# A macaron layer in fp32: row additions off VectorE, and its small work regrouped within the attention units

## The chip, the cores and the metric

The kernel runs on one core of a Trainium2 chip. A core has five engines that run side by side, each with its own instruction queue: TensorE (PE in the profile; its weight loads are PEld), VectorE (DVE), ScalarE (ACT), GpSimd (POOL) and SyncE (SP, which here only issues DMAs). The metric is the time of one execution on the device in microseconds (us); lower is better. Before the change the median of three runs is 1375.16 us (1372.16 to 1376.97).

## What is computed

Tokens come as x of shape 8 x 1024 x 256 in fp32. The layer is

```
x = x + 0.5 * moe(layernorm(x))     # 8 experts, top 2, capacity 1.25 N / E = 1280
x = x + attention(layernorm(x))     # 16 heads of 16, causal, softmax, with Wq, Wkv, Wo and biases
x = x + 0.5 * moe(layernorm(x))
```

An expert that more tokens choose than its capacity is dropped as a whole (keep = counts <= cap, and 2 N choices over 8 experts average 2048). The kernel therefore computes gates, top-2 choices and counts for both expert layers while it does the attention, and branches to code for the expert layers only if some expert fits. With these inputs that code is not run: the time is the time of the attention with the two gates beside it.

## The kernel before, in words

The function `attention` (L686 on) handles 8 batches of 1024 tokens. A batch has four head groups of four heads each; one head group of one batch is a **unit** u, 32 in all, with b, g = divmod(u, 4). The text below calls the four units of a batch g = 0, 1, 2, 3. A unit has 24 **steps**, k = 0 to 23 (loop at L1237). In each step TensorE computes, interleaved,

- two blocks of exponent scores of unit u (`sc`, `e_steps`): ScalarE takes their exp into `pT`, GpSimd zeroes the part above the diagonal with an affine select where the block lies on it, and two or three steps later TensorE multiplies them with the values (`pav`, `values`, L927);
- two blocks of the same scores of unit u + 1 in the other orientation (`sm`, `m_steps`, L852), of which only the row maximum is wanted. Each block is read by VectorE: in steps 0 to 7 and 16 to 23 by a reduction with the causal mask, recorded as `CUSTOM_DVE_ANT_0` and `DVE_READ_ACCUMULATOR2_ANT`, whose sizes run 512, 512, 384, 384, 256, 256, 128, 128 columns; in steps 8 to 15 by a plain `TENSOR_REDUCE` of 512 columns into `first`.

All `sc` and `sm` blocks take turns on six PSUM banks (`score`, L700): a step asks for four, in the order sc, sm, sc, sm. A bank is free for the next block once ScalarE or VectorE has read it. So the second `sm` block of a step can start only when VectorE has read the first `sm` block of the step before.

Everything else is done beside these steps by generators held in `Beside` (L53 on). A generator yields a number (go on so many steps later), or PIECE, QK or REST (go on where TensorE has room for a piece of work). Those that matter here:

- `prepare(b)` (L732) loads a batch and takes layernorm statistics tile by tile with `ln_stats` (`bn_stats`, `bn_aggr`); `enter(b)` normalises on GpSimd (`xn_a`) and transposes.
- `values_of` (L774): per tile of 128 tokens one product `pv` with 264 columns, 256 values and 8 gate logits. ScalarE copies the values to `vaug`, VectorE the logits.
- `leave(b, hf)` (L974): half a batch leaves the attention. Per tile a product `px` with 264 columns; VectorE adds it to the residual row in `xa`; the statistics of the new row are queued in `light`, one taken per step; then the half goes to HBM. It runs in the units g = 0 and g = 1 of the next batch.
- `residual(b)`: four GpSimd additions of the output bias to the residual. `gate_first(b)` and `regate(b)`: the choices (`choose`, L339) for the first and the second expert layer, 20 or 21 small VectorE instructions with one exp on ScalarE, spread over steps by `yield 1`.

Instructions on TensorE, VectorE, ScalarE and GpSimd are kept in the order in which the code issues them (`InOrder`, L27): an instruction that waits holds up everything behind it on its engine. SyncE's DMAs wait in their own order.

Before unit 0 there is an **opening** (L1130 on): x of batch 0 and the weights are loaded, statistics are taken, GpSimd computes the reciprocal deviation `rstd_a`, two halves are normalised, transposed and projected (`project`, L823, which packs heads with eight DMAs per half), and the `sm` blocks of unit 0 run alone. At the **end** (L1290) the last half of batch 7 leaves and the last counts decide the branch.

Of the kernel before, what the change touches and what calls it, by code (L numbers as in the profile page):

```python
# [10 lines left out]
F32 = mybir.dt.float32  # L11
# [91 lines left out]
def macaron_kernel(  # L103
# [112 lines left out]
    def weights(pool, bank, matmul, transpose):  # L216
# [18 lines left out]
        gpsimd.tensor_scalar(bkqT[64:], bkqT[64:], QSCALE, None, ALU.mult)  # L235

# [102 lines left out]
    def choose(rp, tag, n, lg):  # L339
        def new(name, shape=(P, n, E), dt=F32):  # L340
            return rp.tile(list(shape), dt, tag=f"{name}{n}", name=f"{name}_{tag}")

        def over_e(a):
            return a.unsqueeze(2).to_broadcast([P, n, E])

        mx = new("mx", (P, n))
        vector.tensor_reduce(mx, lg, AX.X, ALU.max)
        lc = new("lc")
        vector.tensor_tensor(lc, lg, over_e(mx), ALU.subtract)
        prob = new("prob")  # L350
        yield 1
        scalar.activation(prob, lc, AF.Exp)
        yield 1
        cand = new("cand")
        ohs = [new(f"oh{k}") for k in range(2)]

        def lowest(oh):
            vector.tensor_tensor(cand, cand, iota_e.unsqueeze(1).to_broadcast([P, n, E]), ALU.add)
            first = new("first", (P, n))
            vector.tensor_reduce(first, cand, AX.X, ALU.min)  # L360
            vector.tensor_tensor(oh, cand, over_e(first), ALU.is_equal)

# [12 lines left out]
        vector.scalar_tensor_tensor(key, key, 1e30, lc, ALU.mult, ALU.min)  # L375
        vector.scalar_tensor_tensor(key, ohs[0], -1e32, key, ALU.mult, ALU.add)
        yield 1
        best = new("best", (P, n))
        vector.tensor_reduce(best, key, AX.X, ALU.max)
        vector.tensor_tensor(cand, key, over_e(best), ALU.is_equal)  # L380
        yield 1
        vector.tensor_scalar(cand, cand, -100.0, None, ALU.mult)
        lowest(ohs[1])
        yield 1
        return prob, ohs
# [300 lines left out]
    def attention(run_no, src, dst, gate0, logits, tally):  # L686
# [3 lines left out]
        with stack:  # L690
# [41 lines left out]
            def prepare(b):  # L732
                xb = xbs[b] = ap.tile([P, TB, D + E], F32, tag="xa", name=f"xa{b}", bufs=3)
                nc.sync.dma_start(out=xb[:, :, :D], in_=src[b].rearrange("(j p) d -> p j d", p=P))
                yield 2
                st, mv = ln_tiles(f"a{b}")
                for j in range(TB):
                    ln_stats(xb, j, st, mv)
                    yield 2
                stds[b] = norm.tile([P, TB], F32, tag="std", name=f"std{b}")  # L740
                lns[b] = mv, ln_rstd(mv, f"a{b}", stds[b])
                yield 2
# [31 lines left out]
            def values_of(b, apart, j0=0, j1=TB):  # L774
# [7 lines left out]
                for j in range(j0, j1):  # L782
# [16 lines left out]
                    vector.tensor_copy(lg[:, j, :], pv[:, D : D + E])  # L799
# [23 lines left out]
            def project(u, parts=(0, 512)):  # L823
                b, g = divmod(u, NG)
                xnT = xnTs[b]
                for s0 in parts:
# [17 lines left out]
                    for k in range(8):  # L844
                        r = 32 * (k % 4)
                        nc.sync.dma_start(  # L846
# [125 lines left out]


            def leave(b, hf):  # L974
# [28 lines left out]
                for i in range(TB // 2):  # L1003
# [13 lines left out]
                    vector.tensor_tensor(xb[:, j, :], px[:, : D + E], xb[:, j, :], ALU.add)  # L1017
                    light.append(lambda j=j: ln_stats(xb, j, *gate_lns[b]))
# [84 lines left out]
            def regate(b, j0, j1):  # L1103
# [5 lines left out]
                yield 3  # L1109
# [34 lines left out]
            for qT in qTs:  # L1144
                gpsimd.memset(qT, 0.0)
            for vaug in vaugs:
                gpsimd.memset(vaug[:, :, : NH * VW].rearrange("p t (h r) -> p t h r", r=VW)[:, :, :, HD:], 1.0)
                gpsimd.memset(vaug[:, :, NH * VW :], 1.0)
# [9 lines left out]
            for j0 in (0, HT):  # L1158
                for j in range(j0, j0 + HT):
                    ln_stats(xb, j, st, mv)  # L1160
                part = slice(j0, j0 + HT)
                rstds.append(ln_rstd(mv[:, part, :], f"a0_{j0}", stds[0][:, part]))
            for hf in range(2):
# [12 lines left out]
            owed, light, last, ons = deque(), deque(), [], {}  # L1176
# [3 lines left out]
            for u in range(-1, NU):  # L1180
                b, g = divmod(u, NG)
                if u == 0:
                    beside.finish(opening)
                    preparing = beside.add(prepare(1))
                    opening = beside.add(values_of(0, 0, HT, TB), first=True)
                    projecting = beside.add(project(2))
                    beside.add(chain((PIECE,), turning, residual(0), gate_first(0)))
# [3 lines left out]
                if u >= 0 and g == 3 and b + 1 < B:  # L1191
                    beside.finish(valuing)
                    valuing = beside.add(chain(values_of(b + 1, 0, HT, TB), residual(b + 1)))
# [4 lines left out]
                if g == 3 and u >= 0:  # L1198
                    if b + 2 < B:
                        preparing = beside.add(prepare(b + 2))  # L1200
# [13 lines left out]
                for k in range(0, STEPS, 2) if u == NU - 1 else ():  # L1214
# [10 lines left out]
                    if k == 0:  # L1225
                        beside.add(divided(b, 1, 8, 12, ons[1][:, 1], (1, 3, 3, 3)))
                    if k == 0:
# [9 lines left out]
                for k in range(STEPS) if 0 <= u < NU - 1 else ():  # L1237
# [14 lines left out]
                    if light:  # L1252
# [8 lines left out]
                    if g == 0 and b and k == 9:  # L1261

                        beside.add(gate_first(b))
                    if g == 0 and b and k == 2:
                        beside.add(chain(leave(b - 1, 1), regate(b - 1, 0, TB)))
# [25 lines left out]
            for k, _ in enumerate(leave_last(B - 1, 1, last.pop(), (scalar.copy, vector.tensor_copy))):  # L1291
                for _ in range(3 if k < 2 else len(beside.works) * STEPS):
# [66 lines left out]
```

## Time and profile before

| what | value |
|---|---|
| median of 3 runs | 1375.16 us |
| the profiled execution | 1375.38 us, of it span 1373.6 us |
| TensorE busy | 1336.6 us (97%) |
| VectorE busy | 1038.2 us (76%) |
| ScalarE busy | 785.5 us (57%) |
| GpSimd busy | 398.1 us (29%) |
| residual additions on VectorE (`xa<-px`) | 64 of 427 ns |
| logit copies on VectorE (`logits<-pv`) | 64 of 159 ns |
| statistics on VectorE (`st_a`, `st_g`; `mv_a`, `mv_g`) | 128 of 420 ns; 128 of 182 ns |

The span runs from the first to the last instruction of the core. A busy share is the time in which at least one instruction of the engine is under way. Matmuls overlap and their ends are modelled, so an interval counted as busy for TensorE can still hold a wait. A chain of waits follows the work that ended last back to what released it.

### The profile page before, as it was taken

To read this page: it belongs to the slowest core of one execution; us is meant where nothing else is said; L and a number is where in the kernel's file an instruction comes from. 1 tells how busy PE (TensorE), PEld (TensorE's weight loads), DVE (VectorE), ACT (ScalarE), POOL (GpSimd) and SP (SyncE) were. 2 spreads that over 40 slices of the span, in tenths; PEclk is the share of its full clock that TensorE was granted. 3 is DMA by queue.
4 is the path that set the end of the run, shared out by engine and by line. 5 is a ranking of instruction groups with operands and counts; after the bars stand their busy time and mean duration, and the time that the engine had idled before them with its cause. 6 is when DMAs were issued, how large, how long until landed. Compare 5 with 4: busy or idle time off the path is not lost.

```text
span 1373.6 us, 51244 instructions
## 1 busy us (share of the span) xinstructions
PE 1336.6 (97%) x20664; PEld 445.5 (32%) x20664; DVE 1038.2 (76%) x3417; ACT 785.5 (57%) x1790; POOL 398.1 (29%) x720
## 2 busy tenths in 40 slices
PE   6999999999999999999999999999999999999994
PEld 2333333333333333333333333333333333333331
DVE  3877677887787877877788777788777787787854
ACT  3256665565655565556665656656665556555562
POOL 3034114341235213152141411424123521312321
PEclk9899999999999999999999999999999999999997
DMA  4011111121121211212021211212112111121101
GB/s 142 18 27 42 42 43 56 55 72 42 53 65 49 83 31 48 74 52 77 21 58 60 84 46 37 60 57 73 42 54 58 53 49 34 50 74 42 60 27 34
DMA packets 67024, 73.73 MB, mean 54 GB/s; under 512 B 24688, under 2 KB 42232, under 8 KB 66776
## 3 DMA queue, kind: packets, MB, share of 16 engines
q1 hardware_dynamic: 65688, 69.82, 17.4%
q8 instruction: 165, 2.70, 0.8%
q14 instruction: 83, 0.68, 0.2%
q10 hardware_dynamic: 1088, 0.53, 0.1%
HBM read 26.87 MB, written 26.20 MB: 39 GB/s over the span
## 4 chain that ended last, share of the span: by engine, by line
PE 95%; DVE 3%; DMA 1%; issue 1%; POOL 0%; ACT 0%; SPq 0%; ACTq 0%; POOLq 0%
PE sc L37 42%; PE pav L37 24%; PE sm L37 10%; PE pq L37 9%; PE pv L37 5%; PE px L37 4%; PE pta L37 1%; DVE sm L37 1%; DMA bkqT<-in_L_attn_bq_dram 0%; DVE cand_g L37 0%; SPq L846 0%; PE px_last L37 0%; DVE top L37 0%; DVE first_g L37 0%; DVE oh_g L37 0%
## 5 line engine op out<-in xcount | busy, mean ns | idle before, releaser
L37 ACT ACTIVATE pT<-sc 128x512 f32<-128x512 f32 (+3 forms) x1536 | 668.9, 488 | 518.1 <-PE sm L37 381.4
L37 PE MATMUL sm<-kT,qT 32*64 32x512 f32 (+3 forms) x6144 | 752.8, 510 | 4.2 <-DVE top L37 2.2
L37 PE MATMUL sc<-qT,kT 32*64 32x512 f32 (+3 forms) x6144 | 693.8, 507 | 0.0
L37 DVE TENSOR_REDUCE first<-sm 128x1 f32<-128x512 f32 x512 | 328.7, 685 | 123.3 <-PE sm L37 122.6
L37 POOL TENSOR_SCALAR_AFFINE_SELECT pT<-pT 128x256 f32<-128x256 f32 x512 | 207.6, 408 | 735.4 <-ACT pT L37 734.9
L37 PE MATMUL pav<-pT,vaug 128*32 128x256 f32 (+2 forms) x5120 | 381.8, 370 | 2.2 <-POOL pT L37 1.5
L37 DVE CUSTOM_DVE_ANT_0 sm<-sm,causal 128x256 f32<-128x256 f32 (+3 forms) x512 | 241.8, 514 | 90.8 <-PE sm L37 80.3
L37 DVE CUSTOM_DVE_ANT_0 sm<-sm,causal,first 128x256 f32<-128x256 f32 (+3 forms) x512 | 261.4, 556 | 54.3 <-PE sm L37 48.5
L37 PEld LDWEIGHTS sc<-qT,kT 32*64 32x64 f32 x6144 | 183.1, 130 | 345.9 <-ACT pT L37 266.8
L37 PEld LDWEIGHTS sm<-kT,qT 32*64 32x64 f32 x6144 | 210.8, 130 | 33.4 <-DVE top L37 21.5
L37 PEld LDWEIGHTS pav<-pT,vaug 128*32 128x32 f32 x5120 | 102.5, 108 | 362.3 <-issue 282.7
L37 DVE DVE_READ_ACCUMULATOR2_ANT top<- 128x1 f32 x1024 | 145.5, 142 | 0.0
L37 PE MATMUL pq<-xnT,wkqT 128*32 128x512 f32 x1024 | 136.5, 608 | 1.3 <-ACT xnT L37 1.3
L37 PE MATMUL pv<-wvT,xnT 128*32 128x264 f32 x1024 | 81.1, 391 | 0.0
L37 PE MATMUL px<-woT,on 128*32 128x264 f32 x960 | 76.3, 390 | 0.0
L37 POOL TENSOR_SCALAR xn_a<-xa,mv_a,rstd_a 128x256 f32<-128x256 f32 x56 | 67.5, 1221 | 0.0
L37 ACT ACTIVATE packed<-pq,bkqT 128x512 f32<-128x512 f32 x64 | 45.4, 710 | 11.7 <-PE pq L37 11.7
L37 POOL TENSOR_TENSOR xa<-xa,bo_all 128x528 f32<-128x528 f32 x32 | 41.8, 1308 | 14.3 <-issue 13.7
L37 POOL TENSOR_TENSOR on<-on,inv 128x512 f32<-128x512 f32 (+1 forms) x32 | 40.3, 1282 | 14.1 <-DMA inv<-inv_d 14.1
L37 PEld LDWEIGHTS pq<-xnT,wkqT 128*32 128x32 f32 x1024 | 25.9, 110 | 55.5 <-issue 52.0
L37 PEld LDWEIGHTS pv<-wvT,xnT 128*32 128x32 f32 x1024 | 29.6, 110 | 41.8 <-ACT att L37 18.9
L37 PEld LDWEIGHTS px<-woT,on 128*32 128x32 f32 x960 | 27.3, 109 | 37.3 <-ACT att L37 11.4
(122 smaller groups left out, 430.8 us busy)
## 6 DMA issues: line engine op xcount, KB each, us to landing
att_d<-att SPq DMA_DIRECT2D x62, 256.0 KB
kT<-packed SPq DMA_DIRECT2D x256, 32.0 KB
qT<-packed SPq DMA_DIRECT2D x256, 32.0 KB
out_dram<-xa SPq DMA_DIRECT2D x16, 512.0 KB
on<-att_d SPq DMA_DIRECT2D x30, 256.0 KB
inv<-inv_d SPq DMA_DIRECT2D x30, 256.0 KB
xa<-in_L_attn_x_dram SPq DMA_DIRECT2D x7, 1024.0 KB
xa<-in_L_attn_x_dram SPq DMA_DIRECT2D x2, 512.0 KB
```

Of the source, the lines that this page charges most:

```text
L37: i = call(*args, **kwargs)
```

## The change

1. `leave`: ScalarE copies `px` to a tile `row` in SBUF (4 buffers), and GpSimd adds it to `xa`, one tile per step in steps 8 to 16, or when the half leaves. The statistics are queued once the addition is issued and taken only in steps 8 to 15 of g = 1 and g = 2.
2. `values_of`: ScalarE copies the logits.
3. The small work gets units of its own, and steps 8 to 15: `prepare` of batch 2 and later waits 32 steps after its load and then takes a tile a step (in g = 0); `gate_first(b)` moves from g = 0, k = 9 to g = 3, k = 8 of its batch (batch 7: the last unit); `regate(b - 1)` moves from behind the second `leave` to g = 2, k = 9; `residual(b)` moves from g = 3 of the batch before to g = 0, k = 9. `choose` and `regate` lose one and two waiting steps.
4. Opening: GpSimd's scaling of the bias `bkqT`, three of four fills of `qT` and the fills of `vaug` move behind the two `rstd_a`; four of the eight packing DMAs per half of unit 0 are issued by ScalarE.
5. End: the last `leave_last` lets fewer steps of other work pass (1 instead of 3 at its first stop).

TensorE's instructions stand in the same order before and after.

```diff
-        gpsimd.tensor_scalar(bkqT[64:], bkqT[64:], QSCALE, None, ALU.mult)
...
         scalar.activation(prob, lc, AF.Exp)
-        yield 1
...
-            def prepare(b):
+            def prepare(b, wait, apart):
...
-                yield 2
+                yield wait
                 st, mv = ln_tiles(f"a{b}")
                 for j in range(TB):
                     ln_stats(xb, j, st, mv)
-                    yield 2
+                    yield apart
...
-                    vector.tensor_copy(lg[:, j, :], pv[:, D : D + E])
+                    scalar.copy(lg[:, j, :], pv[:, D : D + E])
...
-                        nc.sync.dma_start(
+                        (nc.scalar if u == 0 and k < 4 else nc.sync).dma_start(
...
+            def add_row():
+                xb, j, row, stats = adds.popleft()
+                gpsimd.tensor_tensor(xb[:, j, :], row, xb[:, j, :], ALU.add)
+                light.append(lambda: ln_stats(xb, j, *stats))
...
-                    vector.tensor_tensor(xb[:, j, :], px[:, : D + E], xb[:, j, :], ALU.add)
-                    light.append(lambda j=j: ln_stats(xb, j, *gate_lns[b]))
+                    row = ap.tile([P, D + E], F32, tag="row", name=f"row{b}_{j}", bufs=4)
+                    scalar.copy(row, px[:, : D + E])
+                    adds.append((xb, j, row, gate_lns[b]))
+                yield 2
+                while adds:
+                    add_row()
...
                 rstd = ln_rstd(gate_lns[b][1][:, j0:j1, :], f"g{b}_{j0}")
-                yield 3
+                yield 1
...
-            for qT in qTs:
-                gpsimd.memset(qT, 0.0)
...
+            gpsimd.memset(qTs[0], 0.0)
...
+            if gate0 is not None:
+                gpsimd.tensor_scalar(bkqT[64:], bkqT[64:], QSCALE, None, ALU.mult)
+            for qT in qTs[1:]:
+                gpsimd.memset(qT, 0.0)
...
-                    preparing = beside.add(prepare(1))
+                    preparing = beside.add(prepare(1, 2, 2))
...
-                    beside.add(chain((PIECE,), turning, residual(0), gate_first(0)))
+                    beside.add(chain((PIECE,), turning, residual(0)))
...
-                    valuing = beside.add(chain(values_of(b + 1, 0, HT, TB), residual(b + 1)))
+                    valuing = beside.add(values_of(b + 1, 0, HT, TB))
...
-                        preparing = beside.add(prepare(b + 2))
+                        preparing = beside.add(prepare(b + 2, STEPS + 8, 1))
...
                     if k == 0:
                         beside.add(divided(b, 1, 8, 12, ons[1][:, 1], (1, 3, 3, 3)))
+                        beside.add(gate_first(b))
...
-                    if light:
+                    if adds and 8 <= k <= 16:
+                        add_row()
+                    if light and 8 <= k < 16 and g in (1, 2):
                         light.popleft()()
...
-                    if g == 0 and b and k == 9:
-
+                    if g == 3 and k == 8:
                         beside.add(gate_first(b))
                     if g == 0 and b and k == 2:
-                        beside.add(chain(leave(b - 1, 1), regate(b - 1, 0, TB)))
+                        beside.add(leave(b - 1, 1))
+                    if g == 0 and b and k == 9:
+                        beside.add(residual(b))
+                    if g == 2 and b and k == 9:
+                        beside.add(regate(b - 1, 0, TB))
...
-                for _ in range(3 if k < 2 else len(beside.works) * STEPS):
+                for _ in range((1, 3)[k] if k < 2 else len(beside.works) * STEPS):
```

More of the change, by code (lines that the diff above doesn't have):

```diff
@@ L1143, in attention @@
             vaugs = [fixed.tile([P, TB, NH * VW + 32 - VW], F32, name=f"vaug{run_no}_{k}") for k in range(2)]
-            for qT in qTs:
-                gpsimd.memset(qT, 0.0)
-            for vaug in vaugs:
-                gpsimd.memset(vaug[:, :, : NH * VW].rearrange("p t (h r) -> p t h r", r=VW)[:, :, :, HD:], 1.0)
-                gpsimd.memset(vaug[:, :, NH * VW :], 1.0)
+            gpsimd.memset(qTs[0], 0.0)
             for kT in kTs[:2]:
@@ L1162, in attention @@
                 rstds.append(ln_rstd(mv[:, part, :], f"a0_{j0}", stds[0][:, part]))
+            if gate0 is not None:
+                gpsimd.tensor_scalar(bkqT[64:], bkqT[64:], QSCALE, None, ALU.mult)
+            for qT in qTs[1:]:
+                gpsimd.memset(qT, 0.0)
+            for vaug in vaugs:
+                gpsimd.memset(vaug[:, :, : NH * VW].rearrange("p t (h r) -> p t h r", r=VW)[:, :, :, HD:], 1.0)
+                gpsimd.memset(vaug[:, :, NH * VW :], 1.0)
             for hf in range(2):
@@ L1175, in attention @@
             opening = beside.add(chain(some(turning, 2), project(1), values_of(0, 0, 0, HT)))
-            owed, light, last, ons = deque(), deque(), [], {}
+            owed, adds, light, last, ons = deque(), deque(), deque(), [], {}
             STEPS = 24
```

## The prediction

> **What bounds the kernel now.** I read the chain of waits first, then busy times unit by unit, then VectorE in order of time.
>
> ```profile
> PE 95%; DVE 3%; DMA 1%; issue 1%; POOL 0%; ACT 0%; SPq 0%; ACTq 0%; POOLq 0%
> ```
>
> TensorE carries the chain. If it only streamed, nothing done to VectorE could matter outside opening and end. So I compare stretches with the same matmuls. Two lines per unit, steps 0-7 and 8-23, for g = 0, 1, 2, 3 of one batch, then unit 27 (g = 3 without a batch to prepare). Columns: stretch, its length, busy (instructions) of PE, PEld, DVE, ACT, POOL, clock, DMA.
>
> ```profile
> 545.72:557.83 12.11, 12.11 (x213) 4.04 (x209) 8.97 (x37) 7.08 (x19) 6.57 (x12) 1.00 0.17 47
> 557.83:586.90 29.07, 29.07 (x436) 9.10 (x432) 24.72 (x80) 16.01 (x36) 3.25 (x8) 1.00 0.23 70
> 586.90:599.02 12.12, 12.12 (x213) 4.05 (x209) 8.99 (x37) 7.08 (x19) 5.69 (x10) 1.00 0.17 46
> 599.02:629.33 30.31, 29.93 (x452) 10.19 (x448) 23.78 (x70) 18.37 (x40) 15.14 (x19) 1.00 0.27 82
> 629.33:641.56 12.23, 12.23 (x212) 4.15 (x208) 10.03 (x45) 7.44 (x19) 2.96 (x8) 1.00 0.17 46
> 641.56:669.08 27.52, 27.52 (x436) 8.88 (x432) 19.57 (x53) 16.87 (x38) 3.25 (x8) 1.00 0.12 33
> 669.08:681.19 12.11, 12.11 (x212) 4.04 (x208) 9.47 (x41) 7.46 (x20) 3.25 (x8) 1.00 0.17 46
> 681.19:708.96 27.77, 27.77 (x436) 9.06 (x433) 22.05 (x64) 16.87 (x38) 9.55 (x15) 1.00 0.19 54
> ...
> 1159.49:1171.52 12.03, 12.03 (x212) 3.97 (x208) 8.37 (x35) 7.45 (x20) 3.25 (x8) 1.00 0.17 47
> 1171.52:1199.04 27.52, 27.52 (x436) 8.88 (x432) 19.88 (x54) 16.87 (x38) 8.13 (x13) 1.00 0.19 55
> ```
>
> The same 436 matmuls take 27.52 us where VectorE is busy 19.6 and 29.07 where it is busy 24.7, with TensorE "busy" throughout: there are waits hidden inside busy time. VectorE in such a place (g = 0, steps 15 to 17):
>
> ```profile
> 575.91 0.23 DVE L37 TENSOR_TENSOR oh_f<-cand_f,first_f 128x64 f32<-128x64 f32 x1
> 576.06 0.42 DVE L37 TENSOR_TENSOR xa<-px,xa 128x264 f32<-128x264 f32 x1
> 576.40 0.75 DVE L37 CUSTOM_DVE_ANT_0 sm<-sm,causal,first 128x512 f32<-128x512 f32 x1
> ...
> 577.74 0.42 DVE L37 BATCH_NORM_STATS2 st_g<-xa 128x6 f32<-128x256 f32 x1
> 578.19 0.18 DVE L37 BATCH_NORM_AGGREGATE mv_g<-st_g 128x2 f32<-128x6 f32 x1
> 578.29 0.46 DVE L37 TENSOR_TENSOR tally<-tally,oh_f 128x64 f32<-128x64 f32 x2
> 578.66 0.76 DVE L37 CUSTOM_DVE_ANT_0 sm<-sm,causal,first 128x512 f32<-128x512 f32 x1
> ```
>
> No idle time stands before any of them: small work delays the masked reductions, these hold the six banks, and TensorE's next `sm` block waits. Steps 17 and 18 take 2.54 and 2.06 us where their shortest twins take 1.61 and 1.40.
>
> **What can be saved in the units.** Clean halves are 12.03 and 27.52. The waits left in these (0.40 in step 17, 0.26 in step 11) come without small work and stay. For g = 1 I add step by step: the four transposes in steps 16 to 19 make 29.2. Per batch then: g = 0: 0.08 + 1.55 = 1.63; g = 1: 0.09 + 1.11 = 1.2; g = 2: 0.20; g = 3: 0.08 + 0.25 = 0.33. These occur in 7, 7, 7 and 6 units: 11.4 + 8.4 + 1.4 + 2.0 = 23.2. Units 0 and 1 lose 0.34 and 0.46 at `gate_first(0)`, 0.8 more.
>
> **What the moved work costs in its new place.** Off VectorE go 56 residual additions (427 ns; the last 8 `xa<-px`, of `leave_first`, stay) and 64 logit copies (159 ns). The rest is packed into steps 8 to 15. Most last 2.06: reductions are ready 1.18 after the step's start and take 1.29, so 0.77 is free; lateness up to 0.17 costs nothing, as TensorE wants the first reduction (0.69) only 2.10 after that start. Step 10 lasts just 1.63. Pieces from their rows: statistics of a tile 0.60; parts of `choose` 0.45, 0.98, 0.69, 0.73, 0.45, 0.98, 0.46, with the first 0.86 in `regate`.
> - g = 1, eight tiles of statistics: nothing; at 446.40 such a pair lay in a 2.06 step and left 0.22 idle.
> - g = 0, eight tiles: only step 10, where a reciprocal of 0.54 stands too: 0.4 in step 12.
> - g = 3, `gate_first`: 0.98 behind the transpose of step 9 is 0.15 late; ScalarE's exp of 0.26 beside it delays the exps about as much, in parallel; 0.1 later: 0.25.
> - g = 2, `regate`: 0.86 in the short step 10, then 0.98: 0.19 + 0.1; the last 0.98 before the masked step 16: 0.4: 0.7.
> - Unit 30: its additions stay on VectorE and `regate` now falls on them. Steps 8 to 17 need 22.3 of VectorE against 19.0 of TensorE: 3.0, against 0.9 saved in its steps 0 to 3.
>
> Sum of the units: -0.8; g = 0: -11.4 + 6 x 0.4 = -9.0; g = 1: -8.4 - 0.2 (unit 29 lost more); g = 2: 6 x (0.7 - 0.2) = +3.0; unit 30: +2.1; g = 3: -2.0 + 7 x 0.25 = -0.25. Together -13.55. The new waits in it are 2.4 + 4.2 + 1.75 + 3.0 = 11.4; their bounds are 0 and twice as much.
>
> **Where the work goes.** ScalarE: 56 copies of 264 columns at about 0.38 (`vaug<-pv`, 256 columns: 373 ns) and 64 of 8 at about 0.17: +32 on 785. They come 0.2 after a step's end, and its next exps are ready at 1.15: 0.95 of room for 0.38 or 0.54; `pv` and `px` find their bank read as early as before. Cover gone, each copy would hold two exps and a bank. GpSimd: 56 additions at 0.66 (half of 1308 ns for 528 columns), in steps 8 to 16 where it has no selects; beside `enter` (8 x 1.22) or `residual` (4 x 1.31) they sum to 12.4 and 10 us of some 16. In g = 0 `rstd_a` (1.67) precedes the second select of step 17: done about 5.9 after step 16 starts, wanted at 6.3: nothing, 0.4 of slack. Statistics wait for these additions: four older tiles come first, so each has three to four steps: nothing. SyncE: `out_dram` waits on GpSimd instead of VectorE, two steps later; behind it stand the row maxima, wanted a unit later. The load of the next batch but one goes to g = 3, its buffer free since g = 2: nothing.
>
> [...] But `first` keeps 685 beside `xn_a` and statistics 420 beside selects, and `choose` has no additions beside it in its new units. By the rows: nothing. [...]
>
> **Opening.**
>
> ```profile
> 9.16 0.25 POOL L37 TENSOR_SCALAR bkqT<-bkqT 64x4 f32<-64x4 f32 x1 [1.12 <-DMA bkqT<-in_L_attn_bq_dram]
> 9.82 1.03 POOL L37 TENSOR_TENSOR rstd_a<-ve_a,half 128x4 f32<-128x4 f32 x1
> 10.89 1.38 DVE L37 TENSOR_SCALAR xn_a<-xa,mv_a,rstd_a 128x256 f32<-128x256 f32 x4 [0.82 <-POOL rstd_a L37]
> ...
> 24.48 2.63 PE L37 MATMUL sm<-kT,qT 32*64 32x512 f32 x12 [0.26 <-DMA qT<-packed]
> ```
>
> Without the bias's DMA ahead of it `rstd_a` is ready before VectorE ends its eighth statistics at 10.06: -0.8. The deferred fills (2.8 of `qT`, 0.8 of `vaug`) end near 16, first wanted after 33. Four DMA issues (4 x 0.63) now stand before ScalarE's last `xnT` copy: second projection +1.0 after -0.8, but `qT` and `kT` are issued side by side, and `sm` starts at 22.8 in one run instead of 23.1 and 24.5: -1.5. From 37 to 55 VectorE never idles: three logit copies gone, -0.5. Together -2.0; the granted clock, 0.5 from 24.5 to 31.4, could make it -5, a worse queue on ScalarE +1.
>
> **End.** `prob_g` now precedes ScalarE's last four exps and waits for VectorE (1347.46): `pav` ends 0.9 later; VectorE then has 1.8 of `choose` before `att_last`, but less after: `normed` 1352.5 instead of 1351.9: +0.6 (0 to 1.2).
>
> Sum: -13.55 - 2.0 + 0.6 = -15.0 on 1375.4 of the profiled execution, which is the median within 0.2: **1360.4**.
>
> **Rivals.**
> 1. The new waits are near zero: 1360.4 - 11.4 = 1349. For it: the pair at 446.40. Against it: pieces of 0.98 exceed 0.77.
> 2. The packed steps cost twice my 11.4: 1371.8, no measurable change or little gain. For it: in g = 0 today 1.3 of waits follow 7.8 of small work, and g = 2 will hold 5.9.
> 3. It doesn't do what it says: TensorE's pace is its own, and the 27.52 against 29.07 has another cause: only opening and end remain, 1375.4 - 2.0 + 0.6 = 1374. Against it: same matmuls, clock 1.00.
> [...]
>
> **How the numbers follow.** About 0.3% (4 us) is what a measurement here can tell from no change. Chances: forecast 0.58 (its own range 1354 to 1367), rival 1 0.18, rivals 2 and 3 together 0.14, half of it within 0.3%, rival 4 0.10. Faster 0.58 + 0.18 + 0.07 = 0.83, same 0.07, slower 0.10. With about 0.1 left out on each side: 1348 (no new waits, a luckier clock in the opening) to 1373 (just past rival 2).
>
> **What would show it.** Right: g = 0 near 39.95 and g = 1 near 41.25 us, masked reductions without small work before them, unit 30 longer, first `sm` run near 22.8. Wrong: statistics far over 0.42, ScalarE's copies delaying exps, selects awaited by `pav`, or g = 2 above 41.

## The result, and the profile after

The changed kernel takes 1355.95 us (median of four runs, 1354.68 to 1356.49) against 1375.7 for the kernel before: ratio 0.9859, 95% interval 0.9839 to 0.9879. The forecast was 1360.4, range 1348 to 1373. The profiled execution has a span of 1354.1 us, 19.5 less than the 1373.6 before. The chain that ended last still runs on TensorE:

```profile
PE 95%; DVE 3%; DMA 1%; ACT 0%; issue 0%; ACTq 0%; POOL 0%; SPq 0%; DVEq 0%
```

The same stretches as in the forecast's table, two lines per unit (steps 0-7 and 8-23) for g = 0, 1, 2, 3 of one batch (units 12 to 15), then steps 8-23 of unit 27. Columns: stretch, its length, busy (instructions) of PE, PEld, DVE, ACT, POOL, clock, DMA.

```profile
540.13:552.16 12.03, 12.03 (x212) 3.97 (x208) 8.20 (x34) 7.46 (x20) 5.68 (x10) 1.00 0.17 47
552.16:579.75 27.59, 27.59 (x436) 8.96 (x432) 23.42 (x67) 16.90 (x38) 13.55 (x20) 1.00 0.26 73
579.75:591.79 12.04, 12.04 (x212) 3.98 (x208) 8.20 (x34) 7.47 (x20) 5.67 (x10) 1.00 0.17 46
591.79:620.99 29.20, 29.20 (x452) 9.94 (x448) 22.54 (x64) 19.24 (x42) 15.80 (x20) 1.00 0.17 49
620.99:633.03 12.04, 12.04 (x212) 3.97 (x209) 8.21 (x34) 7.53 (x21) 3.25 (x8) 1.00 0.17 45
633.03:660.75 27.72, 27.72 (x437) 9.07 (x433) 23.10 (x73) 17.22 (x42) 5.18 (x10) 1.00 0.24 72
660.75:672.78 12.03, 12.03 (x212) 3.97 (x208) 8.20 (x34) 7.52 (x21) 3.25 (x8) 1.00 0.17 46
672.78:700.30 27.52, 27.52 (x436) 8.89 (x432) 23.04 (x71) 17.19 (x42) 3.25 (x8) 1.00 0.20 55
...
1153.48:1181.06 27.58, 27.58 (x436) 8.70 (x432) 23.03 (x71) 17.17 (x42) 3.25 (x8) 1.00 0.19 55
```

Nearly every half-unit now has its clean length (12.03 and 27.52; 29.2 for g = 1). VectorE is not less busy for it: in g = 3 it went from 22.05 to 23.04 us while the half became 0.25 shorter. In the second half of g = 0 it still holds 23.42.

VectorE at the place that the forecast showed, steps 15 to 17 of g = 0, in order of time:

```profile
567.84 1.29 DVE L37 TENSOR_REDUCE first<-sm 128x1 f32<-128x512 f32 x2 [0.22 <-PE sm L37]
569.04 0.42 DVE L37 BATCH_NORM_STATS2 st_a<-xa 128x6 f32<-128x256 f32 x1
569.49 0.18 DVE L37 BATCH_NORM_AGGREGATE mv_a<-st_a 128x2 f32<-128x6 f32 x1
569.89 0.76 DVE L37 CUSTOM_DVE_ANT_0 sm<-sm,causal,first 128x512 f32<-128x512 f32 x1 [0.22 <-PE sm L37]
...
571.51 0.76 DVE L37 CUSTOM_DVE_ANT_0 sm<-sm,causal,first 128x512 f32<-128x512 f32 x1
```

Now idle time of 0.22 us stands before a reduction: VectorE waits for TensorE, not the other way. Note also that the next instruction starts 1.20 us after a pair of reductions that is printed as lasting 1.29.

Where the 19.5 us of the profiled span lie, by aligning the same matmuls of both traces:

| stretch | change, us | the forecast |
|---|---|---|
| opening, to the start of unit 0 | +1.1 | -2.0 |
| units 0 and 1 | -0.4 | -0.8 |
| g = 0, seven units | -11.0 | -9.0 |
| g = 1, seven units | -8.5 | -8.6 |
| g = 2 (six units) | -0.3 | +3.0 |
| g = 3, seven units | -1.9 | -0.25 |
| unit 30 | +1.8 | +2.1 |
| unit 31 and the end, to the last VectorE instruction | +0.9 | +0.6 |
| after the last VectorE instruction | -1.15 | 0 |

The last row is hardly the change: this tail was 7.6 us in the profiled execution of before and 6.4 to 7.1 in all thirteen others of this study, 6.4 too in offload_only, which leaves the end as it was.

The opening after:

```profile
8.02 1.03 POOL L37 TENSOR_TENSOR rstd_a<-ve_a,half 128x4 f32<-128x4 f32 x1
10.06 1.35 DVE L37 TENSOR_SCALAR xn_a<-xa,mv_a,rstd_a 128x256 f32<-128x256 f32 x4
17.70 2.54 ACTq L844 DMA_DIRECT2D kT<-packed  x4
20.28 0.59 ACT L37 COPY xnT<-pta 128x512 f32<-128x512 f32 x1 [2.13 <-DMA kT<-packed]
20.92 3.64 PE L37 MATMUL pq<-xnT,wkqT 128*32 128x512 f32 x16 [2.54 <-ACT xnT L37]
24.49 2.01 PE L37 MATMUL sm<-kT,qT 32*64 32x512 f32 x16
25.34 3.74 ACTq L844 DMA_DIRECT2D kT<-packed  x4
30.14 0.59 ACT L37 COPY wvT<-pt_w 128x512 f32<-128x512 f32 x1
30.29 3.54 PE L37 MATMUL pq<-xnT,wkqT 128*32 128x512 f32 x16 [1.46 <-ACT wvT L37]
```

The second projection before:

```profile
19.89 1.92 PE L37 MATMUL pq<-xnT,wkqT 128*32 128x512 f32 x16 [0.68 <-ACT xnT L37]
```

The normalisation starts at 10.06 instead of 10.89, as forecast. ScalarE's last `xnT` copy stands 2.13 us behind its own four DMA issues, and the second projection waits 2.54 for it and starts at 20.92, 1.0 later than before. It then takes 3.64 us instead of 1.92 (the granted clock is 0.5 from 19.95 to 26.77), and the first `sm` run follows at 24.49, not at 22.8. ScalarE's second four issues (25.34 to 29.08) hold up its copies of the weights `wvT`, for which the third projection waits another 1.46.

### The profile page after: what moved, and what is told of

It is laid out like the page before. It is cut to its first block, busy times and chain, and to the rows that moved or that the text cites. A ratio compares the mean times of both kernels' runs of the same rounds, so it can differ in the third digit from the quotient of the medians.

```text
span 1354.1 us, 51543 instructions
## 1 busy us (share of the span) xinstructions
PE 1319.6 (97%) x20664; PEld 439.3 (32%) x20664; DVE 1020.4 (75%) x3297; ACT 809.2 (60%) x1910; POOL 440.5 (33%) x776
## 4 chain that ended last, share of the span: by engine, by line
PE 95%; DVE 3%; DMA 1%; ACT 0%; issue 0%; ACTq 0%; POOL 0%; SPq 0%; DVEq 0%
PE sc L37 42%; PE pav L37 24%; PE pq L37 9%; PE sm L37 8%; PE pv L37 5%; PE px L37 4%; PE pta L37 1%; DVE first L37 1%; DMA xa<-in_L_attn_x_dram 0%; ACTq L844 0%; PE px_last L37 0%; DVE cand_g L37 0%; DVE xa L37 0%; DVE st_g L37 0%; POOL rstd_g L37 0%
## 5 line engine op out<-in xcount | busy, mean ns | idle before, releaser
L37 PE MATMUL sm<-kT,qT 32*64 32x512 f32 (+3 forms) x6144 | 733.1, 510 | 0.0
L37 PEld LDWEIGHTS sm<-kT,qT 32*64 32x64 f32 x6144 | 205.2, 130 | 17.8 <-DVE first L37 6.3
L37 POOL TENSOR_TENSOR xa<-row,xa 128x264 f32<-128x264 f32 x56 | 41.7, 745 | 66.8 <-ACT row L37 66.8
```

Source lines behind the costliest of these rows:

```text
L37: i = call(*args, **kwargs)
```

## The experiments

Twelve kernels; a ratio is to the kernel before, run on the same chip. The lengths of units below are read from one profiled execution each. Where the code of a unit is the same, its mean length came out within 0.08 us from kernel to kernel, so these lengths resolve what the medians, which spread over 1 to 5 us, can't.

| kernel | median, us | lowest to highest | ratio, 95% interval |
|---|---|---|---|
| regroup_only | 1356.14 | 1353.76 to 1357.30 | 0.9861, 0.9846 to 0.9876 |
| offload_only | 1368.17 | 1367.40 to 1368.32 | 0.9943, 0.9929 to 0.9957 |
| adds_on_vector | 1355.38 | 1354.83 to 1356.96 | 0.9853, 0.9838 to 0.9868 |
| stats_twice | 1371.53 | 1369.94 to 1373.30 | 0.9970, 0.9960 to 0.9980 |
| stats_masked | 1359.43 | 1356.51 to 1360.67 | 0.9872, 0.9857 to 0.9887 |
| gp_add_beside | 1366.62 | 1363.57 to 1367.60 | 0.9929, 0.9908 to 0.9950 |
| gp_scalar_beside | 1355.95 | 1354.16 to 1358.02 | 0.9859, 0.9842 to 0.9876 |
| open_sync | 1352.90 | 1352.33 to 1354.94 | 0.9838, 0.9824 to 0.9851 |
| opening_before | 1354.96 | 1353.32 to 1355.43 | 0.9845, 0.9831 to 0.9858 |
| three_edits | 1354.02 | 1352.24 to 1356.75 | 0.9839, 0.9825 to 0.9852 |
| first_off | 1353.94 | 1352.48 to 1354.32 | 0.9839, 0.9826 to 0.9852 |
| first_off_end | 1353.52 | 1351.30 to 1354.35 | 0.9835, 0.9822 to 0.9849 |

### Which part gains: the places or the engines

**regroup_only** is the kernel before with part 3 of the change alone, and the rule of part 1 that the statistics of new rows wait for steps 8 to 15 of g = 1 and g = 2.

```diff
-            def prepare(b):
+            def prepare(b, wait, apart):
...
-                        beside.add(chain(leave(b - 1, 1), regate(b - 1, 0, TB)))
+                        beside.add(leave(b - 1, 1))
+                    if g == 0 and b and k == 9:
+                        beside.add(residual(b))
+                    if g == 2 and b and k == 9:
+                        beside.add(regate(b - 1, 0, TB))
...
-                    if light:
+                    if light and 8 <= k < 16 and g in (1, 2):
...
```

> The kernel before with the regrouping alone: additions and logit copies on VectorE, opening and end as before. If the places of the small work are the whole gain of the units: units 2 to 28 run as in the changed kernel (39.6, 41.2, 39.8, 39.6 for g = 0 to 3), 20.3 us shorter than before, unit 30 as in the changed kernel, together 1355 to 1357. If it needs the work off VectorE as well: g = 0 and g = 1 stay above 40.5 and 42, and the time is over 1362.

Measured 1356.14. Its units take 39.67, 41.24, 39.79 and 39.56 us (g = 0 to 3, means without units 2 and 29, which have less to do) against 39.64, 41.26, 39.75 and 39.58 in the changed kernel. From the start of unit 2 to that of unit 29 it is 20.2 us shorter than before; the changed kernel is 20.3 shorter. The regrouping alone is the whole gain of the units.

**offload_only** is the kernel before with parts 1 and 2 alone, without that rule on the statistics.

```diff
-                    vector.tensor_tensor(xb[:, j, :], px[:, : D + E], xb[:, j, :], ALU.add)
-                    light.append(lambda j=j: ln_stats(xb, j, *gate_lns[b]))
+                    row = ap.tile([P, D + E], F32, tag="row", name=f"row{b}_{j}", bufs=4)
+                    scalar.copy(row, px[:, : D + E])
+                    adds.append((xb, j, row, gate_lns[b]))
...
-                    vector.tensor_copy(lg[:, j, :], pv[:, D : D + E])
+                    scalar.copy(lg[:, j, :], pv[:, D : D + E])
...
```

> The kernel before with its additions and logit copies off VectorE, all other small work where it was. If a step is as long as its reductions and small work together, an addition taken out helps where it was stacked with statistics and choices: up to 0.43 in step 14, 17 or 18 of g = 0 and in steps 22 and 23 of g = 1, 0.5 to 1 us in each of 14 units: 1362 to 1369. If only the regrouping gains: 1375 to 1376. If statistics now wait for GpSimd: above 1376.

Measured 1368.17, 7.2 us less than before. g = 1 takes 41.68 instead of 42.44, g = 0 only 40.92 instead of 41.21, g = 2 even 0.2 more. So taking work off VectorE helps where the places are bad. The parts don't add up: with the regrouping there is nothing left for the offload to save.

**adds_on_vector** is the changed kernel with the 56 additions back on VectorE.

```diff
-                    row = ap.tile([P, D + E], F32, tag="row", name=f"row{b}_{j}", bufs=4)
-                    scalar.copy(row, px[:, : D + E])
-                    adds.append((xb, j, row, gate_lns[b]))
-                yield 2
-                while adds:
-                    add_row()
+                    vector.tensor_tensor(xb[:, j, :], px[:, : D + E], xb[:, j, :], ALU.add)
+                    light.append(lambda j=j: ln_stats(xb, j, *gate_lns[b]))
+                yield 2
```

> The changed kernel with the 56 residual additions back on VectorE where the product ends, no copy on ScalarE, no addition on GpSimd; the regrouping stays. If the place decides, only one addition per half falls in a masked step (step 4, 0.08 lost before): about +1 us, 1357. If taking work off VectorE is what gained: 56 x 0.427 = 24 us at most come back, in proportion some 10 or more, so over 1366. [...]

Measured 1355.38; its units take 39.70, 41.24, 39.77 and 39.60. VectorE beside two pairs of reductions in g = 0, in order of time:

```profile
559.96 0.41 DVE L37 BATCH_NORM_STATS2 st_a<-xa 128x6 f32<-128x256 f32 x1
560.40 0.18 DVE L37 BATCH_NORM_AGGREGATE mv_a<-st_a 128x2 f32<-128x6 f32 x1
560.50 0.40 DVE L37 TENSOR_TENSOR xa<-px,xa 128x264 f32<-128x264 f32 x1
560.82 1.28 DVE L37 TENSOR_REDUCE first<-sm 128x1 f32<-128x512 f32 x2
```

Statistics and addition fill the room between two pairs of reductions exactly (0.86 us from 559.96 to the next pair); in g = 0 steps 11, 12 and 17 grow by 0.01 to 0.03 in the mean, no other. 24 us of additions (56 x 0.427) on or off VectorE make no difference that can be measured here.

### What a place costs

**stats_twice** takes each pair of statistics of the new rows twice in its step.

```diff
-                light.append(lambda: ln_stats(xb, j, *stats))
+                light.append(lambda: (ln_stats(xb, j, *stats), ln_stats(xb, j, *stats)))
```

> The changed kernel with each pair of statistics of the new rows taken twice in its step (the second gives the same numbers): 1.2 us beside two reductions in steps 8 to 15 of g = 1. If the room beside them is about 0.85 us a step, as the changed kernel's trace suggests (2.06 less 1.21), the eight steps lose 2.6 to 3 per unit: 18 to 21 us in 7 units, so 1374 to 1377. By the 0.77 of the forecast: 3.3 per unit, 1379. If TensorE sets the pace of these steps whatever VectorE does: 1356.

Measured 1371.53, 15.6 above the changed kernel. g = 1 takes 43.56 instead of 41.26; steps 12 to 15 each 2.40 instead of 2.06. One period of it on VectorE, in order of time:

```profile
603.24 1.25 DVE L37 TENSOR_REDUCE first<-sm 128x1 f32<-128x512 f32 x2
604.41 0.41 DVE L37 BATCH_NORM_STATS2 st_g<-xa 128x6 f32<-128x256 f32 x1
604.86 0.18 DVE L37 BATCH_NORM_AGGREGATE mv_g<-st_g 128x2 f32<-128x6 f32 x1
605.08 0.43 DVE L37 BATCH_NORM_STATS2 st_g<-xa 128x6 f32<-128x256 f32 x1
605.54 0.18 DVE L37 BATCH_NORM_AGGREGATE mv_g<-st_g 128x2 f32<-128x6 f32 x1
605.64 1.25 DVE L37 TENSOR_REDUCE first<-sm 128x1 f32<-128x512 f32 x2
```

1.17 for the reductions and 1.23 for the small work are the 2.40 of the step, with no idle time: VectorE sets the pace, and TensorE follows it. So a step of this kind lasts 2.06, or about 1.2 plus its small work if that is longer. The room is 2.06 less 1.17 to 1.21, so 0.85 to 0.89, and work beyond it is paid in full. The total lies under the expected 1374 to 1377: steps 8 to 10 kept their length, and steps 11 to 16 lost 2.3 us a unit, not 2.6 to 3.

**stats_masked** takes the same statistics once, in steps 16 to 23.

```diff
-                    if light and 8 <= k < 16 and g in (1, 2):
+                    if light and 16 <= k < 24 and g in (1, 2):
```

> The changed kernel with the statistics of the new rows taken in steps 16 to 23 of g = 1 instead of steps 8 to 15; same instructions, other places. If the place decides (masked reductions hold the banks), steps 20 to 23, whose reductions leave some 0.4 us for a pair of 0.60, lose 0.3 to 0.6 each and steps 16 to 19, which the transposes make longer, 0 to 0.2: 1.2 to 3.2 per unit, 8 to 22 us in 7 units, so 1364 to 1378. If only VectorE's total counts: 1356.

Measured 1359.43, 3.5 above the changed kernel and far under the forecast 8 to 22. g = 1 takes 41.72 instead of 41.26 and g = 2 0.10 more. Of the eight steps only the last two grew (1.10 and 1.31 in the mean instead of 0.95 and 0.99). Steps 16 to 19 are long there because of the transposes (8.4 us together, 6.7 in other units), which leaves room. Unit 29, a g = 1 without a batch to enter and so without transposes, shows it: it lost 1.16, in steps 18 to 23. A masked step is not a bad place in itself; it has less room.

### GpSimd beside VectorE

In unit 30 of the changed kernel two small instructions of the choices last 0.97 and 0.98 us; their usual time is 0.22. VectorE and GpSimd in order of time:

```profile
1276.91 1.27 POOL L37 TENSOR_TENSOR on<-on,inv 128x512 f32<-128x512 f32 x1 [0.80 <-DMA inv<-inv_d]
1277.30 0.97 DVE L37 TENSOR_TENSOR lc_g<-logits,mx_g 128x64 f32<-128x64 f32 x1
...
1281.55 1.28 POOL L37 TENSOR_TENSOR on<-on,inv 128x512 f32<-128x512 f32 x1 [3.37 <-DMA inv<-inv_d]
1281.93 0.98 DVE L37 TENSOR_TENSOR prob_g<-prob_g,sm_g 128x64 f32<-128x64 f32 x1
```

Each lasts from its turn until shortly after GpSimd's product ends (1278.18 and 1282.83). The next two kernels put spare work of GpSimd beside the choices of g = 2, batches 0 to 5, where it otherwise has none.

```diff
                     lg, xb[:, j0:j1, D:], rstd[:, :n].unsqueeze(2).to_broadcast([P, n, E]), ALU.mult
                 )
+                if b < B - 2:
+                    spare = ap.tile([P, D + E], F32, tag="spare", name=f"spare{b}", bufs=1)
+                    gpsimd.tensor_tensor(spare[:, :E], lg[:, 0], lg[:, 1], ALU.add)
+                    for k in range(13):
+                        gpsimd.tensor_tensor(spare, xb[:, k % TB, :], xb[:, (k + 1) % TB, :], ALU.add)
```

> The changed kernel with 13 spare additions on GpSimd (two inputs in SBUF, 264 columns, 0.745 us each, result unused) beside the choices in steps 10 to 15 of g = 2, batches 0 to 5. If an addition on GpSimd shuts out VectorE's small instructions with two SBUF inputs until it ends, as lc and prob (0.97 and 0.98 instead of 0.22) suggest beside the product on<-on,inv in unit 30, eight such instructions per unit wait some 0.4 each on average: the steps with more than 0.85 of small work lengthen, 2 to 4 per unit, 12 to 24 us in 6 units, so 1368 to 1380. If the two engines don't exclude each other: 1356.

Measured 1366.62, 10.7 above the changed kernel, a little under the expected 12 to 24. g = 2 takes 41.53 instead of 39.75 (6 x 1.78 = 10.7); steps 13 and 15 take 2.95 instead of 2.06. GpSimd, then VectorE, in order of time:

```profile
643.24 9.06 POOL L37 TENSOR_TENSOR spare<-xa 128x264 f32<-128x264 f32 x11
644.93 0.82 DVE L37 TENSOR_TENSOR cand_g<-cand_g,iota_e 128x64 f32<-128x64 f32 x1
645.78 0.22 DVE L37 TENSOR_REDUCE first_g<-cand_g 128x8 f32<-128x64 f32 x1
...
649.92 0.83 DVE L37 SCALAR_TENSOR_TENSOR key_g<-key_g,lc_g 128x64 f32<-128x64 f32 x1
650.78 0.79 DVE L37 SCALAR_TENSOR_TENSOR key_g<-oh_g,key_g 128x64 f32<-128x64 f32 x1
```

Instructions with two inputs in SBUF last up to some 0.8 instead of 0.22 where an addition is under way when their turn comes; `lc_g` and `prob_g`, which come just before one starts, keep their 0.22. The reduction with one input keeps its 0.22 beside an addition, but `cand_g<-lc_g` and `key_g<-prob_g`, a `TENSOR_SCALAR` with one input each, last 0.37 instead of 0.18. GpSimd hardly pays. Its 78 additions (durations in ns, shortest, median and longest):

```profile
L37 POOL TENSOR_TENSOR spare<-xa x78: 739/747/799, 319.2 to 1139.2; 128x264 f32<-128x264 f32 x78
```

The 0.82 from one to the next (9.06 / 11) is the distance from one start to the next. Only 12 of the 78 took 0.77 to 0.80.

**gp_scalar_beside** has eight instructions with one input instead of the 13 additions.

```diff
-                    for k in range(13):
-                        gpsimd.tensor_tensor(spare, xb[:, k % TB, :], xb[:, (k + 1) % TB, :], ALU.add)
+                    for k in range(8):
+                        gpsimd.tensor_scalar(spare, xb[:, k % TB, :], 0.5, 1.0, ALU.mult, ALU.add)
```

> The same place, and instead 8 spare instructions on GpSimd with one input in SBUF (a scale and a constant, 264 columns, about 1.25 us each). If only GpSimd's additions with two inputs exclude VectorE: 1356. If any GpSimd instruction does: as long as the kernel with the spare additions or longer, since each one holds longer.

Measured 1355.95, the changed kernel's time; g = 2 takes 39.75. They lasted 0.41 each instead of the expected 1.25, so they cover 638.0 to 642.0 only, GpSimd first here, then VectorE:

```profile
638.02 3.98 POOL L37 TENSOR_SCALAR spare<-xa 128x264 f32<-128x264 f32 x8
641.86 0.23 DVE L37 TENSOR_TENSOR prob_g<-prob_g,sm_g 128x64 f32<-128x64 f32 x1
```

The two-input instructions of the choices beside them keep 0.23. Only `prob_g` is a plain test: in each of the six units it comes while the last of the eight is under way (641.59 to 642.00 here). Two others start before GpSimd's instruction or together with it, and there it is GpSimd that takes longer, 0.43 and 0.50. So this form did not shut out VectorE in six cases. That is not so of every GpSimd instruction with one input: in the kernel before, `cand_g<-lc_g` lasts 0.365 beside a select (one input) and `cand_f<-lc_f` 0.185 with nothing beside it.

So GpSimd's additions make no unit of the changed kernel slower, although they held VectorE up above (some 0.8 instead of 0.22): in units 1 to 29 the change puts statistics (one input) beside the additions and the choices (two inputs) into units where GpSimd has nothing with two inputs to do. The kernel offload_only shows the other case: there `tally` and `oh_f` stand beside `xa<-row,xa` and lost 2.98 and 2.85 us in seven units (in unit 12 the pair of `tally` takes 0.91 instead of 0.46, one `oh_f` 0.63 instead of 0.22). In the changed kernel no small instruction of VectorE is longer than usual by a third or more in units 2 to 29.

### The opening

**open_sync** is the changed kernel with all of unit 0's packing DMAs on SyncE.

```diff
-                        (nc.scalar if u == 0 and k < 4 else nc.sync).dma_start(
+                        nc.sync.dma_start(
```

> The changed kernel with all packing DMAs of unit 0 issued by SyncE. If ScalarE's issuing of DMAs cost the opening (its xnT copy waits 2.13 us behind four issues, the projection after it starts at 20.92), that projection starts near 19.1, the first sm run near 22.3, and unit 1 near 98.7 instead of 101.0: 1353.6. If side-by-side issue gained what the forecast gave it (1.5): unit 1 near 102.5, 1357.5. If the half clock from 19.95 to 26.77 is what made the opening late: unit 1 moves less than 0.5 either way.

Measured 1352.90, 3.05 under the changed kernel; the intervals of the two ratios overlap a little, so the traces have to show the cause.

```profile
19.23 0.58 ACT L37 COPY xnT<-pta 128x512 f32<-128x512 f32 x1 [0.29 <-PE pta L37]
19.87 1.92 PE L37 MATMUL pq<-xnT,wkqT 128*32 128x512 f32 x16 [0.68 <-ACT xnT L37]
```

The last `xnT` copy comes at 19.23 instead of 20.28, the projection at 19.87 instead of 20.92 (expected: 19.1), and `sm` starts at 22.74. Unit 1 starts at 97.55; not all of the 3.5 us is the edit, as the table below shows.

**opening_before** also puts the bias and the fills back ahead of the deviation.

```diff
-                        (nc.scalar if u == 0 and k < 4 else nc.sync).dma_start(
+                        nc.sync.dma_start(
...
-            gpsimd.memset(qTs[0], 0.0)
+            for qT in qTs:
+                gpsimd.memset(qT, 0.0)
+            for vaug in vaugs:
+                gpsimd.memset(vaug[:, :, : NH * VW].rearrange("p t (h r) -> p t h r", r=VW)[:, :, :, HD:], 1.0)
+                gpsimd.memset(vaug[:, :, NH * VW :], 1.0)
...
```

> The changed kernel with the opening as before: SyncE issues all packing DMAs, and the bias and the fills stand ahead of the reciprocal deviation; the logit copies stay on ScalarE. If putting off the fills is worth the 0.8 by which the first deviation comes earlier: 0.8 above the kernel that differs by the DMAs alone (1352.9), so 1353.7, unit 1 near 98.4. If the fills were hidden anyway: 1352.9.

Measured 1354.96, unit 1 at 99.99, against expected 1353.7 and 98.4. Three kinds of opening ran under several kernels. Grouped by how long the granted clock was 0.5 before 35 us, the start of unit 1 in the profiled executions:

| opening | 3.4 us of half clock | 6.8 us | 10.2 us |
|---|---|---|---|
| as changed (ScalarE issues) | 98.49, 99.36, 99.75 | 100.41, 101.63 | 101.03 |
| fills put off, SyncE issues | 97.55 | 98.89, 99.34, 99.51 | |
| as before (logit copies on either engine) | 98.96 | 99.93, 99.99, 100.52 | |

In the column with the most entries ScalarE's issuing costs 1.8 (101.02 against 99.25), putting off the fills gains 0.9 (100.15 against 99.25), and the opening as changed is 0.9 later than that of before. Without the grouping the means are 100.1, 98.8 and 99.9, with ranges that overlap. From the first column to the second 3.4 us more of half clock go with 1.2 to 1.8, as much as any of the edits.

Two waits come with ScalarE's issuing in all six of its executions and in none of the eight others: the second projection waits 2.4 to 2.8 us for the `xnT` copy (0.7 in the others), and the third projection waits 1.2 to 2.0 for `wvT`. The half clock is not independent of the edit, either. In five of the six it began between 19.95 and 22.73, so that the second projection took 2.6 to 3.6 us; in the eight others it never began before 23.90, and that projection took 1.92. In the sixth, gp_scalar_beside, it began at 28.29:

```profile
20.04 1.92 PE L37 MATMUL pq<-xnT,wkqT 128*32 128x512 f32 x16 [2.54 <-ACT xnT L37]
21.89 1.11 PE L37 MATMUL sm<-kT,qT 32*64 32x512 f32 x16
```

Whether TensorE's idle time ahead of the projection brings the half clock on was not tried. If it does, the grouping takes part of the edit's cost for chance.

### Unit 30 and the end

**three_edits** has SyncE issue the DMAs, takes the choices of batch 6 out of unit 30, starts the others at k = 8, and restores the stops of the end.

```diff
-                        beside.add(gate_first(b))
+                        beside.add(chain(gate_first(b), regate(b - 1, 0, TB)))
...
-                    if g == 2 and b and k == 9:
+                    if g == 2 and 0 < b < B - 1 and k == 8:
...
-                for _ in range((1, 3)[k] if k < 2 else len(beside.works) * STEPS):
+                for _ in range(3 if k < 2 else len(beside.works) * STEPS):
```

> The changed kernel with three places mended: packing DMAs on SyncE; the choices of the last batch but one in unit 31 instead of unit 30, those of the others one step earlier (k = 8); the end's stops as before (3 and 3 steps). If the losses are where the trace shows them: 3.1 from the opening, 2.6 from unit 30, 0.2 in each of 5 units g = 2, 0.9 at the end, so 1348.4. If unit 30's additions alone fill its steps: 1351.

Measured 1354.02 instead of 1348.4. Against open_sync's trace: unit 1, after the same opening code, started 2.0 later (the half clock lasted 6.8 us, not 3.4). Unit 30 became 2.1 shorter, somewhat less than expected. Unit 31 and the end became 4.1 longer: the choices there stand in VectorE's order ahead of `att_last`, `normed` and `on`, and two of TensorE's transposes wait 2.7 us for `att_last` (1.2 in open_sync). Starting at k = 8 made step 11 of g = 2 take 2.65 instead of 2.32, while steps 17 to 22 lost less: 39.90 instead of 39.75. No piece of it was free.

**first_off** leaves the choices and instead takes the eight additions of unit 30 off VectorE (DMAs on SyncE as well).

```diff
                     matmul_cols(px[:, : D + E], on[:, 0, i * P : (i + 1) * P], woT[:, 0, :])
-                    vector.tensor_tensor(xb[:, j, :], px[:, : D + E], xb[:, j, :], ALU.add)
+                    row = ap.tile([P, D + E], F32, tag="row", name=f"row{b}_{j}", bufs=4)
+                    scalar.copy(row, px[:, : D + E])
+                    adds.append((xb, j, row, None))
...
```

> The changed kernel with packing DMAs on SyncE and the eight additions of unit 30 copied by ScalarE and added by GpSimd too, the choices left where the change put them. If unit 30 is long because 8 additions of 0.43 stand on VectorE beside the choices in steps 11 to 18, it gets 2.6 shorter, and the time is 2.6 under that of the kernel with the DMAs alone: 1350.3. If the length comes from the choices alone, or GpSimd's additions delay the selects of steps 16 to 23: 1353.

Measured 1353.94, not 1350.3. Against open_sync TensorE is 0.8 ahead in step 17 of unit 30, 0.3 at the start of unit 31 and nothing from its step 6 on. GpSimd took part of it: `lc_g` still lasts 0.95 beside `on<-on,inv`, and `key_g` 0.70 beside the new `xa<-row,xa`.

**first_off_end** adds the old stops of the end.

```diff
-                for _ in range((1, 3)[k] if k < 2 else len(beside.works) * STEPS):
+                for _ in range(3 if k < 2 else len(beside.works) * STEPS):
```

> The same, and the end's stops as before (3 and 3 steps instead of 1 and 3). If the exp of the last choices standing ahead of the last four exps of the attention costs what the trace shows (the last product with the values 0.9 later): 0.9 less, 1349.4. If the shorter stop pays for itself at the last choices: no change, 1350.3.

Measured 1353.52, 0.4 less, within the spread of either. The exp `prob_g` still stands ahead of ScalarE's last four exps (1325.93 before 1326.07), so the stops didn't put it there. regroup_only agrees: with the old stops, it takes 47.0 us from the start of unit 31 to the last VectorE instruction, as the changed kernel does, against 46.1 before and 45.7 in offload_only. So the loss at the end comes with part 3, not with part 5; which piece of part 3 brings it (`gate_first` in the last unit, or the waiting steps that `choose` and `regate` lost) was not tried. None of these last kernels is measurably better than open_sync.

## Why the prediction was right or wrong

The time fell into the range, 4.5 us under the forecast in the profiled execution (-19.5 against -15.0 from 1375.4). That it came so near is in part luck: three groups of units came out 7.0 better, the opening 3.1 worse, and 1.15 of the gain lies in the tail, which nobody forecast. Step by step:

- **What bounds.** Right. TensorE follows VectorE: stats_twice lengthens the steps by what its work exceeds the room by.
- **Saved in the units, 23.2 and 0.8.** Right. The halves went to the clean lengths that the forecast took from the table, and the sum for g = 1 came within 0.1; of the 0.8 of units 0 and 1 half came. The forecast took the change as one and did not ask which part buys this: part 3 does, and moving the additions off VectorE, which gives the change its name, adds nothing to it.
- **New waits, 11.4: mis-sized, the main error.** In g = 0, g = 2 and g = 3 the sums came to 7.0 less (2.0 + 3.3 + 1.7). The failed step is the room: 0.77, from 2.06 less the 1.29 of a pair of reductions as the trace prints it. The next instruction starts 1.17 to 1.21 after the pair's start, so the room is 0.85 to 0.89. The pieces shrink in the same way: those of 0.98 and 0.69 take 0.88 and 0.62 from start to start in unit 15 (685.47 to 686.35, 679.47 to 680.09), and the steps around them keep their length. stats_twice shows the room in g = 1; that it accounts for each of the three groups is worked out, not tried. Of the new waits there, 0.08 a unit in g = 0 and some 0.2 in g = 2 are left; the latter lie in steps 17 to 22 and are gone in three_edits, where the choices start a step earlier. The rival with new waits near zero was the better account of g = 0, 2 and 3; the one with twice the waits is out.
- **Unit 30, +3.0 less 0.9.** Right in size (+1.8 in all), partly by luck: half wrong in cause. The forecast counted VectorE's work against TensorE's; but 1.5 us of VectorE's time is `lc_g` and `prob_g` shut out by `on<-on,inv`. It depends on where these meet: in regroup_only only one instruction was held there (0.75 instead of 0.18), and its unit 30 took 39.57, 0.9 more than before, against 40.49 in the changed kernel. The forecast held that `choose` has no additions beside it, and overlooked that it has these products beside it there.
- **GpSimd's additions beside VectorE.** "By the rows: nothing" was right for units 1 to 29 and for this change, though as a reading of the hardware too weak. Statistics and the small reduction kept their time beside additions (0.42 and 0.22). Instructions with two inputs in SBUF did not: `cand_g` and `key_g` took 0.79 to 0.83 instead of 0.22 beside additions, `lc_g` 0.97 beside `on<-on,inv`. Beside the one-input instructions of gp_scalar_beside `prob_g` kept its time (0.23 in six cases). Why two `TENSOR_SCALAR` with one input took 0.37 instead of 0.18 beside additions, where the reduction with one input kept its 0.22, no run here shows. The chances give slower 0.10; that GpSimd's additions lengthen the changed kernel, no run shows either: adds_on_vector, without the 56 of them, took 1355.38 against 1355.95.
- **Durations of the moved work.** The addition on GpSimd takes 0.745, not 0.66; the copy 0.38 as taken. Neither delays a select or an exp by anything that the units show.
- **Opening, -2.0: wrong sign (+1.1), just outside the bounds given (-5 to +1).** The 0.8 of the deviation is right, and so is the second projection, +1.0 (20.92 after 19.89). Two steps failed. The first is "`sm` starts at 22.8", which gives this projection the 1.92 us of before: it lasted 3.64 at half clock, and `sm` started at 24.49. The forecast had the half clock where it lay before, from 24.5 on. In gp_scalar_beside, with the same opening and a later half clock, `sm` started at 21.89. The second is the wait for `wvT`: the forecast counted the first four issues on ScalarE and put the second four at nothing, and they cost TensorE a wait of 1.46. How the 3.1 divide between the two is not shown.
- **End, +0.6.** +0.9, within its bounds.
- **The rival that TensorE's pace is its own** is out: the same 436 matmuls take 27.59 instead of 29.07 in g = 0.

## What to carry to other kernels

Add up, step by step, what the engine that frees the banks has to do, and compare it with the step: here small work was free up to the room (0.85 to 0.89 us in a step of 2.06) and paid in full beyond it (1.23 made 2.40 in stats_twice), so spreading it can be worth more than taking it away (here 19.2 us against 7.2, and nothing more from both). Read the room from the start of one instruction to the start of the next, not from printed durations, which overlap (a pair printed as 1.29 was followed after 1.17 to 1.21 here). Before giving an engine DMAs to issue (four took ScalarE 2.54 us here), look at what it has to do next, and before giving GpSimd two-input work, at what VectorE does beside it (0.22 became 0.8 in gp_add_beside).

## What was not expected of the hardware

- **The clock of the opening differs from execution to execution.** Before 35 us the granted clock was 1.0 or 0.5. It was 0.5 from 24.5 to 31.4 us in the kernel before, and from 19.95 to 26.77 and from 30.2 to 33.6 in the changed kernel: 10.2 us in all, where others with the same opening had 3.4 to 6.8. The first half-clock stretch began between 20 and 28 us (19.95 in the changed kernel, 28.29 in gp_scalar_beside). What sets its beginning and its length, no run here shows. The mean clock of the same 10 us in the changed kernel and in open_sync (0.66 and 0.83 in the column after POOL):

```profile
20.00:30.00 10.00, 7.91 (x54) 2.04 (x54) 3.49 (x11) 3.08 (x4) 0.00 (x0) 0.66 0.20 42
```

```profile
20.00:30.00 10.00, 8.80 (x66) 2.83 (x66) 4.18 (x13) 3.32 (x5) 0.00 (x0) 0.83 0.23 50
```

- **GpSimd and VectorE held each other up, unequally**: VectorE's 0.22 became up to 0.83 beside GpSimd's additions (gp_add_beside). An addition that met a two-input instruction of VectorE took 0.77 to 0.82 instead of 0.745 (12 of 78 in gp_add_beside; 7 of 56 in offload_only, beside `tally`).
